# Layer 0's output products of blocks 2 to 7 moved behind its last units and into layer 1, its last half units put in single banks, early steps of the choice cut from ten to six, a scaling split between ScalarE and GpSimd

## The chip, the cores and the metric

The kernel runs on one core of a Trainium2 chip. A core has a matrix engine (TensorE, PE in the profile), a vector engine (VectorE, DVE), an activation engine (ScalarE, ACT), a general engine (GpSimd, POOL) and an engine that issues transfers (SyncE, SP). Each runs its own list of instructions in order; semaphores order the engines against one another. Matmuls write into PSUM, which has eight banks of 128 x 512 fp32 values; everything else is held in SBUF or in device memory. The metric is device time in microseconds, the median over runs.

## The reference

The program is a sequence of four residual layers over x, 8 x 512 tokens of 128 fp32 features. The change touches layer 0 and the start of layer 1. Layer 0 has an attention without softmax and a mixture of experts for each head:

```python
# layer 0, attention: three branches, batch norm over all tokens, a sigmoid as spike
q, k, v = (sigmoid(4.0 * (batch_norm(norm(x) @ W.T) - 1.0)) for W in (Wq, Wk, Wv))
qk = heads(q * k) * 8 ** -0.5                 # 16 heads of 8
x = x + merge(qk @ (heads(v).T @ heads(v))) @ Wp.T + bp

# layer 0, experts: 8 heads of 16 features, 16 experts, the two best are taken
t = (norm(x) @ Wm + bm).reshape(-1, 16)       # one row for each token and head
w = softmax(t @ expert_emb); topw, topi = top_k(w, 2)
hmid = gelu(einsum('td,edi->tei', t, W1) + b1)   # 16 -> 64, all 16 experts
eo = einsum('tei,eio->teo', hmid, W2) + b2       # 64 -> 16
comb = (take(eo, topi) * topw).sum(1).reshape(..., 128)
x = x + comb @ Wo + bo
```

Layer 1 begins with a layer norm of x and a linear attention (q, k through exponentials, a sum over k and v, its product with q, an output product), followed by a feed-forward part. Layers 2 and 3 (softmax attention and low-rank experts; a convolution-like attention and a gated feed-forward part) come after and are not touched.

## The kernel before, in words

The 4096 tokens are 8 blocks of 512 (`NB = 8`, `TB = 512`), and a block is 4 tiles of 128 tokens (`J = 4`, `P = 128`). `x[b]` holds a block with tokens on partitions. The order of the work is written out by hand: each engine does its instructions in the order in which the program names them.

Layer 0 has three parts, by time in the profile. *Pass one* (0 to 41 us) normalizes x, makes the three branches and their statistics. *Pass two* (42 to 101 us) is a software pipeline over the blocks: `run` takes a list of stages with a lag each and calls each with the block number plus its lag. Its `scale(b, J)` makes the normalized input of the experts, four ACT instructions of 128 x 128, one for each tile (`scaled`, L743); with the default `own=3` it would do three on ACT and the fourth on POOL (L349), as pass one does. `turned` transposes the result, `hidden` makes h, `logits` takes the products with the expert vectors, and `exponentials` writes exp(logits) into acc. `biased` (L352) and the product of two spikes (L392) are on POOL.

The *experts* (103 to 382 us) are 128 units, one for each block b and expert e, with n = 16 b + e. The first half of a unit (`first_half`) makes hmid of 64 features for all 8 heads: four matmuls, one into a single bank with the tag "first" and three into a tile of three banks (two such tiles, `threes`, taken in turn), and two gelus on ACT (L569 of 128 x 512, L570 of 128 x 1536). The second half (`second_half`), two units later, multiplies back to 16 features for each head (PE), adds the bias and multiplies by the gate of that expert (DVE, L582, tile pr), and POOL adds pr to acc (L588). For e = 0, DVE writes acc itself. The gates, nonzero for two experts of each token and head, come from `choice(b)`: twelve steps on DVE and POOL (L448 to L474), ending with a transpose and four transfers of `gates[b]` to device memory on SP (L477). `spread(b, k)` then loads the gates of four experts into a tile gs with a copy on each of the 16 partitions of a head (eight transfers, L550; three such tiles). While the units run, `side` lets one step of the next block's choice, and of some preparations for layer 1 (`places`, `first_norms`), be done in each unit; in units 0 and 1 it does five steps each, so that the choice for block 1 is done early.

`finish(b)` makes layer 0's output: acc of a block times Wo, four 128 x 128 matmuls over tokens (`by_token`, L253), and adds it to x[b] on DVE (`add_to_residual`, L274). It runs in the fifth unit of the next block. The product goes to the bank that is the first of the three-bank tile which this unit doesn't use (`banks["own"]`). The very last pr isn't added to acc; it is a second term of the last finish, which thus has eight products. After the last unit the two remaining second halves use the second and third bank of `threes[0]`, and then finish(7) runs.

`layer1` starts with some memsets on POOL (L1245 to L1254; `nought` is a tile of zeros that is copied to device memory), and goes over the blocks with its own list of stages (`stages`, above the loop at its end): transposes (`turn_`), projections (`project_q`, `project_kv`), maps with exponentials (`q_map`, `k_map`), `gather` (the sum over k and v), `attend`, `output`, then the feed-forward part with a lag. PE, ACT and DVE take their shares of a stage in the order of this list. PSUM then has four single banks (tag "one") and two pairs. `late()` holds layers 2 and 3.

SBUF pools matter for where acc lies: `once` lives for layer 0 only, `first` is held until layer 1's end.

Of the kernel before, what the change touches and what calls it, by code (L numbers as in the profile page):

```python
# [17 lines left out]
F32 = mybir.dt.float32  # L18
# [7 lines left out]
P = 128  # L26
D = 128
# [137 lines left out]
def body(ctx, tc, dram, spans, x_in, ib, it, ic, ei, out):  # L165
# [111 lines left out]
        return t[:, j * P : (j + 1) * P]  # L277


    def layer0():  # L280


# [5 lines left out]
        with ExitStack() as st:  # L288
# [4 lines left out]
            emb = once.tile([P, 8, 16], F32, tag="emb", name="emb")  # L293
            emb_f = emb.rearrange("p h e -> p (h e)")
            h = once.tile([P, NB, TB], F32, tag="h", name="h")
            acc = once.tile([P, NB, TB], F32, tag="acc", name="acc")
            depth = once.tile([P, NB, TB], F32, tag="depth", name="depth")
            gates = [tc.dram_tile([P, TB], F32, name=f"gates{b}") for b in range(NB)]
            G = J * 8
# [40 lines left out]
            def stats(b):  # L340
                l0[b]["by"] = stats_of(x[b], J)

            def scale(b, own=3):
                l0[b]["xn"] = xn = norm.tile([P, J, D], F32, tag="xn", name="xn")
                nb, rs = l0[b]["by"]
                scaled(xn, x[b], (nb, rs), own)
                for j in range(own, J):
                    r1, n1 = rs[:, j : j + 1], nb[:, j : j + 1]
                    nc.gpsimd.tensor_scalar(xn[:, j, :], x[b][:, j, :], r1, n1, ALU.mult, ALU.add)  # L349

            def biased(b, bias):
                nc.gpsimd.tensor_tensor(  # L352
# [84 lines left out]
                nc.vector.tensor_tensor(by_expert(depth, b), pl3, over(mx), ALU.subtract)  # L437

            def exponentials(b):
                nc.scalar.activation(acc[:, b, :], depth[:, b, :], AF.Exp)  # L440

            def choice(b):


                d, ex = by_expert(depth, b), by_expert(acc, b)
                place, top, sm = small("place"), small("top"), small("sm")
                eq, one, left = big("eq"), big("one"), big("left")
                nc.vector.scalar_tensor_tensor(eq, d, 0.0, rank, ALU.is_equal, ALU.mult)  # L448
                yield "V"
                nc.vector.tensor_reduce(place, eq, AX.X, ALU.max)  # L450
                yield "V"
                nc.vector.tensor_tensor(one, eq, over(place), ALU.is_equal)
                yield "V"
                nc.vector.scalar_tensor_tensor(left, one, -1e30, d, ALU.mult, ALU.add)
                yield "V"
                nc.vector.tensor_reduce(top, left, AX.X, ALU.max)
                yield "V"
                nc.vector.tensor_tensor(eq, left, over(top), ALU.is_equal)
                nc.gpsimd.tensor_tensor(eq, eq, rank, ALU.mult)
                yield "V"  # L460
                nc.vector.tensor_reduce(sm, ex, AX.X, ALU.add)
                nc.vector.reciprocal(sm, sm)
                nc.gpsimd.tensor_tensor(ex, ex, over(sm), ALU.mult)
                yield "V"
# [24 lines left out]
            with (  # L489
                tc.tile_pool(name="a0h", bufs=1) as hp,  # L490
                tc.tile_pool(name="a0", bufs=2) as ap,
                psum({"one": 8}),
                tc.manual_schedule(),
            ):
                hs = [hp.tile([P, NB, TB], F32, tag=f"h{k}", name=f"h{k}") for k in range(3)]
                bst = [hp.tile([P, NB, 6], F32, tag=f"bst{k}", name=f"bst{k}") for k in range(3)]

                def run(stages, iterations):
                    for i in iterations:
                        for f, lag in stages:  # L500
                            if 0 <= i + lag < NB:
                                f(i + lag)

                run(
                    (
                        (scale, 2),
                        (stats, 3),
                        (turned, 1),
                        (project, 0),
                        (lambda b: biased(b, "bp"), -2),  # L510
                    ),
                    range(-3, NB + 2),
                )
                keep_clock(22)
                sc, bi = batch_norm()
                expand()
                run(
                    (
                        (turned, -2),
                        (lambda b: scale(b, J), -1),  # L520
                        (turn_v, 3),
                        (logits, -3),
                        (attended, 0),
                        (stats, 0),
                        (spikes, 4),
                        (gram, 2),
                        (gram_out, 1),
                        (hidden, -2),
                        (exponentials, -3),
                        (lambda b: chosen(3), -4),  # L530
                        (lambda b: biased(b, "bo"), -1),
                        (lambda b: keep_clock(6), -3 - NB // 2),
                    ),
                    range(-4, NB + 3),
                )
                chosen(20)
# [36 lines left out]
            def second_half(b, e, hm, gs):  # L573
                po = bank()
                for i in range(4):
                    mm(
                        po[32 * i : 32 * (i + 1), :],
                        w2[:, e, :, :].rearrange("p a o -> p (a o)"),
                        hm[:, i, :],
                    )  # L580
                pr = acc[:, b, :] if e == 0 else wp.tile([P, TB], F32, tag="pr", name="pr")
                nc.vector.scalar_tensor_tensor(  # L582
                    pr, po, f0["b2"][:, e : e + 1], gs, ALU.add, ALU.mult
                )
                if (b, e) == (NB - 1, 15):
                    l0[b]["last"] = pr
                elif e > 0:
                    nc.gpsimd.tensor_tensor(acc[:, b, :], acc[:, b, :], pr, ALU.add)  # L588

            def finish(b):  # L590
                terms = [(lambda j: acc[:, b, j * P : (j + 1) * P], f0["wo"])]
                if "last" in l0[b]:
                    terms.append((lambda j: cols(l0[b]["last"], j), f0["wo"]))
                add_to_residual(b, by_token(terms, None))

            def places():

# [45 lines left out]
            with tc.manual_schedule():  # L643
# [36 lines left out]
                def second(n):  # L680

                    if n >= 2:
                        b, e = units[n - 2]
                        second_half(b, e, hms.pop(n - 2), gs[(n - 2) // 4][:, e % 4, :])
                        fetch(n - 1)
                    for _ in range(1 if n > 1 else 5):
                        side("V", n)

                for n in range(len(units) + 2):
                    first(n)  # L690
                    if n >= len(units):

                        banks["own"] = threes[0][:, 1 + n - len(units), :]
                        second(n)
                        banks.pop("own")
                        continue

                    banks["own"] = threes[(n + 1) % 2][:, 0, :]
                    b, e = units[min(n, len(units) - 1)]
                    if e == 4 and b > 0:  # L700
                        finish(b - 1)
                    else:
                        side("P", n)
                    banks.pop("own")
                    second(n)
                finish(NB - 1)
                n = 1000
                while kinds.get(1) != "end":
                    side("V", n)
# [121 lines left out]
    def layer1():  # L831
# [9 lines left out]
        with tc.tile_pool(name="l1", bufs=2) as wp, tc.tile_pool(name="l1c", bufs=1) as once:  # L841
# [372 lines left out]
            def chosen_put():  # L1214
# [11 lines left out]
                (f_scale, -3),  # L1226
                (q_map, 0),
                (project_kv, 0),
                (z_turn, -7),
                (output, -2),  # L1230
                (k_map, 0),
# [7 lines left out]
            with tc.manual_schedule():  # L1239
# [10 lines left out]
                for k, name in enumerate(("eb1", "eb2")):  # L1250
                    lo, hi = spans["rows"][name]
                    nc.sync.dma_start(ebs[:, k, :], dram["rows"][:, lo:hi].partition_broadcast(P))
                nought = once.tile([P, J, D], F32, tag="nought", name="nought")
                nc.gpsimd.memset(nought, 0.0)  # L1254
                for b in range(1, NB):
                    nc.sync.dma_start(
# [1421 lines left out]
```

## Time and profile before

| what | us |
|---|---|
| median of three runs (lowest, highest) | 1400.63 (1397.15, 1401.19) |
| the profiled execution, its own time | 1393.95 |
| its span | 1392.2 |
| layer 0, pass one and pass two | 0 to 101 |
| layer 0, the experts | 103 to 382 |
| layer 1 | about 384 to 510 |
| layers 2 and 3 | about 510 to 1392 |
| PE, ACT, DVE, POOL busy over the span | 1327.5, 1014.6, 1014.3, 642.4 |

The profiled execution is 0.5% below the median of the runs, so sums made from its rows are compared with its own time. A line of the timeline reads: start, length, engine, line of the kernel, operation, what it writes and reads, its shape, how many instructions the line stands for, and in brackets how long the engine had been idle ahead of it and who ended that. Matmuls of fp32 are issued as several passes, so "x8" stands for four matmuls of 128 x 128. The lines of a stretch give the busy time (and instructions) of PE, weight loads, DVE, ACT and POOL, the granted clock of the matrix engine as a fraction, the busy share of the transfer engines, and GB/s. Lines of waits give the engine and line that waited, for what, the sum, how many times, and the longest.

### The profile page before, as it was taken

The numbers are of one execution on the slowest core, as the hardware profiler recorded it, in microseconds if no ns is written. First come the engines' busy times: TensorE is split into PE (matmuls) and PEld (weight loads), VectorE is DVE, ScalarE is ACT, GpSimd is POOL, SyncE is SP. The second block draws the span as 40 slices with busy tenths as digits, with TensorE's granted clock in tenths as the row PEclk, the third lists the DMA queues.
The fourth block names the chain that finished last, engine by engine and source line by source line (L and its number), as shares of the span: only waits on it lengthen the run. The fifth ranks groups of instructions, "written<-read, shape, count | busy, mean of one in ns | idle before, by whom it ended". The sixth has DMA issues, their size and how long they took to land.

```text
span 1392.2 us, 33106 instructions
## 1 busy us (share of the span) xinstructions
PE 1327.5 (95%) x12935; PEld 706.1 (51%) x12935; DVE 1014.3 (73%) x2148; ACT 1014.6 (73%) x2060; POOL 642.4 (46%) x748
## 2 busy tenths in 40 slices
PE   7889999999989999999999999999999999999997
PEld 3762222222267655547447545555555545555576
DVE  6785556666467778863783778888788797887876
ACT  7869999999978656665684686787767867667632
POOL 6645666666632533330472353353443634424432
PEclk9999999999999999999999999999999999999999
DMA  5019999999681010031211101101011010010000
GB/s 180 1 27 139 141 126 127 132 127 133 85 272 32 28 40 24 16 108 33 60 31 38 45 2 22 30 2 33 20 22 24 9 33 20 19 27 9 2 8 16
DMA packets 100713, 78.14 MB, mean 56 GB/s; under 512 B 52717, under 2 KB 93581, under 8 KB 96206
## 3 DMA queue, kind: packets, MB, share of 16 engines
q1 hardware_dynamic: 98828, 72.10, 28.3%
q0 software_dynamic: 1152, 2.36, 0.6%
q8 instruction: 102, 1.67, 0.6%
q10 hardware_dynamic: 578, 1.57, 0.3%
q14 instruction: 53, 0.43, 0.1%
HBM read 59.03 MB, written 16.97 MB: 55 GB/s over the span
## 4 chain that ended last, share of the span: by engine, by line
PE 52%; ACT 22%; DVE 19%; issue 3%; POOL 2%; DMA 1%; SPq 1%; DVEq 0%; ACTq 0%; POOLq 0%
PE ps L250 41%; PE ps L1556 8%; ACT hm L570 6%; ACT ex L1635 5%; DVE nm L1629 5%; ACT hm L569 3%; ACT prod L2023 2%; PE ps L2206 1%; DVE fa L1395 1%; DVE acc L2009 1%; DVE s L732 1%; ACT h L389 1%; DVE fa L1379 1%; DVE fsc L1374 1%; ACT q L1517 1%
## 5 line engine op out<-in xcount | busy, mean ns | idle before, releaser
L1635 ACT ACTIVATE ex<-ps,nm 128x512 f32<-128x512 f32 x512 | 345.2, 687 | 172.6 <-DVE nm L1629 170.2
L1629 DVE TENSOR_REDUCE nm<-ps 128x2 f32<-128x1024 f32 x256 | 301.1, 1211 | 41.9 <-PE ps L250 41.5
L250 PE MATMUL ps<-q,k 64*64 64x512 f32 (+1 forms) x2240 | 258.3, 565 | 7.4 <-ACT ex L1635 5.4
L250 PE MATMUL ps<-ex,vs 128*64 128x512 f32 x1024 | 233.9, 599 | 1.1 <-DVE sm L1649 1.1
L1650 POOL TENSOR_TENSOR vs<-v,sm 128x256 f32<-128x256 f32 x128 | 78.6, 614 | 296.6 <-DVE sm L1649 269.6
L588 POOL TENSOR_TENSOR acc<-acc,pr 128x512 f32<-128x512 f32 x119 | 165.6, 1391 | 93.8 <-DVE pr L582 85.8
L1556 PE MATMUL ps<-xt,blob_a 64*64 64x512 f32 x912 | 207.8, 589 | 0.5 <-SPq L1523 0.5
L570 ACT ACTIVATE hm<-ps,blob_f 128x1536 f32<-128x1536 f32 x128 | 196.2, 1533 | 0.0
L582 DVE SCALAR_TENSOR_TENSOR pr<-ps,blob_f,gs 128x512 f32<-128x512 f32 x120 | 90.1, 750 | 93.7 <-PE ps L250 72.1
L250 PEld LDWEIGHTS ps<-q,k 64*64 64x64 f32 x2240 | 74.6, 132 | 150.5 <-ACT ex L1635 77.6
L250 PE MATMUL ps<-h,w 32*128 32x512 f32 x1024 | 148.3, 643 | 1.1 <-ACT hm L569 0.6
L250 PEld LDWEIGHTS ps<-ex,vs 128*64 128x64 f32 x1024 | 68.1, 137 | 152.9 <-issue 126.7
L250 PE MATMUL ps<-hm,w 128*32 128x512 f32 x1024 | 136.9, 607 | 2.3 <-DVE pr L582 2.2
L2024 POOL TENSOR_TENSOR acs<-acs,prod 128x512 f32<-128x512 f32 x96 | 124.0, 1292 | 23.9 <-ACT prod L2023 19.4
L1556 PE MATMUL ps<-blob_a,ct 64*64 64x128 f32 x1824 | 118.6, 269 | 0.0
L1556 PE MATMUL ps<-blob_a,xt 64*64 64x128 f32 x1824 | 118.6, 269 | 0.0
L1556 PEld LDWEIGHTS ps<-blob_a,ct 64*64 64x64 f32 x1824 | 106.3, 133 | 0.0
L1635 ACT ACTIVATION_READ_ACCUMULATOR ex<-ps,nm 128x1 f32 x512 | 104.9, 205 | 0.0
L1556 PEld LDWEIGHTS ps<-blob_a,xt 64*64 64x64 f32 x1824 | 103.0, 133 | 0.0
L569 ACT ACTIVATE hm<-ps,blob_f 128x512 f32<-128x512 f32 x128 | 88.0, 687 | 13.3 <-PE ps L250 13.2
L250 PEld LDWEIGHTS ps<-h,w 32*128 32x128 f32 x1024 | 41.0, 184 | 109.1 <-ACT hm L569 100.5
L1556 PEld LDWEIGHTS ps<-xt,blob_a 64*64 64x64 f32 x912 | 61.7, 133 | 32.2 <-issue 28.7
(373 smaller groups left out, 2204.5 us busy)
## 6 DMA issues: line engine op xcount, KB each, us to landing
gs<-gates SPq DMA_DIRECT2D x248, 128.0 KB, 7.4
ht<-turned_h SPq DMA_DIRECT2D x20, 180.0 KB, 3.0
turned_h<-hb SPq DMA_DIRECT2D x40, 88.0 KB, 2.3
blob_f<-in_f SPq DMA_DIRECT2D x1, 2560.0 KB, 9.0
blob_a<-in_a SPq DMA_DIRECT2D x1, 2056.0 KB, 13.5
x<-in_x SPq DMA_DIRECT2D x8, 256.0 KB, 5.8
gates<-turned SPq DMA_DIRECT2D x32, 64.0 KB, 4.7
slots_in<-nought SPq DMA_DIRECT2D x8, 256.0 KB, 4.8
```

Source lines behind the costliest of these rows:

```text
L250: nc.tensor.matmul(out_, lhs, rhs, start=start, stop=stop)
L389: nc.scalar.activation(hk, hk, AF.Sigmoid, bias=bi[:, k : k + 1], scale=sc[:, k : k + 1])
L569: nc.scalar.activation(hm[:, 0, :], p1, AF.Gelu, bias=bias)
L570: nc.scalar.activation(hm[:, 1:, :], p3, AF.Gelu, bias=bias)
L582: nc.vector.scalar_tensor_tensor(pr, po, f0["b2"][:, e : e + 1], gs, ALU.add, ALU.mult)
L588: nc.gpsimd.tensor_tensor(acc[:, b, :], acc[:, b, :], pr, ALU.add)
L1556: ins = nc.tensor.matmul(*args, **kw).ins
L1629: nc.vector.tensor_reduce(nm, ps, AX.X, ALU.max, negate=True)
L1635: nc.scalar.activation(ex[kt][:, i, :], ps[:, i, :], AF.Exp, bias=nm[:, i : i + 1], accum_out=sm[:, kt, i : i + 1],)
L1650: nc.gpsimd.tensor_tensor(vs[:, tiles, :, :], vs_[n][:, tiles, :].rearrange("p j (i n) -> p j i n", i=2), sm[:, tiles, :].unsqueeze(3).to_ ...
L2023: nc.scalar.activation(p, src, AF.Copy, scale=w)
L2024: nc.gpsimd.tensor_tensor(t["acs"], t["acs"], p, ALU.add)
```

## The change

acc is no longer one tile: blocks 0 to 2 have a tile each in layer 0's pool, blocks 3 to 7 one tile, `last_acc`, in the pool that lives through layer 1. `finish` moves out of `layer0` so that layer 1 can call it. finish(0) and finish(1) stay in the fifth unit of the next block; finish(2) runs after the last unit's first half, between the two remaining second halves; finish(3) to finish(7) become a stage of layer 1, one in each of the iterations 0 to 4, after `project_kv`. The last pr is added to acc as the others are. The two remaining second halves use the banks "one" and "first". In units 0 and 1 `side` does four and two steps. `scale` always gives its fourth tile to POOL, in pass two too. The tile of zeros uses a buffer of another tile, "zo".

```diff
+    acc = []
+    last_acc = first.tile([P, NB - 3, TB], F32, tag="acc", name="acc")
+
+    def finish(b):
+        wo = f0["wo"]
+        add_to_residual(b, by_token([(lambda j: cols(acc[b], j), wo)], None))
...
-            acc = once.tile([P, NB, TB], F32, tag="acc", name="acc")
+            acc.extend(once.tile([P, TB], F32, tag=f"acc{b}", name="acc") for b in range(3))
+            acc.extend(last_acc[:, b, :] for b in range(NB - 3))
...
-            def scale(b, own=3):
+            def scale(b):
                 l0[b]["xn"] = xn = norm.tile([P, J, D], F32, tag="xn", name="xn")
                 nb, rs = l0[b]["by"]
-                scaled(xn, x[b], (nb, rs), own)
-                for j in range(own, J):
-                    r1, n1 = rs[:, j : j + 1], nb[:, j : j + 1]
-                    nc.gpsimd.tensor_scalar(xn[:, j, :], x[b][:, j, :], r1, n1, ALU.mult, ALU.add)
+                scaled(xn, x[b], (nb, rs), 3)
+                r1, n1 = rs[:, 3:4], nb[:, 3:4]
+                nc.gpsimd.tensor_scalar(xn[:, 3, :], x[b][:, 3, :], r1, n1, ALU.mult, ALU.add)
...
-                        (lambda b: scale(b, J), -1),
+                        (scale, -1),
...
-                if (b, e) == (NB - 1, 15):
-                    l0[b]["last"] = pr
-                elif e > 0:
-                    nc.gpsimd.tensor_tensor(acc[:, b, :], acc[:, b, :], pr, ALU.add)
-
-            def finish(b):
-                terms = [(lambda j: acc[:, b, j * P : (j + 1) * P], f0["wo"])]
-                if "last" in l0[b]:
-                    terms.append((lambda j: cols(l0[b]["last"], j), f0["wo"]))
-                add_to_residual(b, by_token(terms, None))
+                if e > 0:
+                    nc.gpsimd.tensor_tensor(acc[b], acc[b], pr, ALU.add)
...
-                    for _ in range(1 if n > 1 else 5):
+                    for _ in range((4, 2)[n] if n < 2 else 1):
                         side("V", n)
...
                     if n >= len(units):
-
-                        banks["own"] = threes[0][:, 1 + n - len(units), :]
+                        if n > len(units):
+                            banks["own"] = bank("first")
                         second(n)
+                        if n == len(units):
+                            banks["own"] = threes[0][:, 0, :]
+                            finish(2)
                         banks.pop("own")
                         continue
...
-                    if e == 4 and b > 0:
+                    if e == 4 and 0 < b < 3:
                         finish(b - 1)
...
-                finish(NB - 1)
...
                 (project_kv, 0),
+                (lambda b: b > 2 and finish(b), 3),
                 (z_turn, -7),
...
-                nought = once.tile([P, J, D], F32, tag="nought", name="nought")
+                nought = wp.tile([P, J, D], F32, tag="zo", name="nought")
```

More of the change, by code (lines that the diff above doesn't have):

```diff
@@ L439, in exponentials @@
             def exponentials(b):
-                nc.scalar.activation(acc[:, b, :], depth[:, b, :], AF.Exp)
+                nc.scalar.activation(acc[b], depth[:, b, :], AF.Exp)
             def choice(b):
-                d, ex = by_expert(depth, b), by_expert(acc, b)
+                d = by_expert(depth, b)
+                ex = acc[b].rearrange("p (g e) -> p g e", e=16)
                 place, top, sm = small("place"), small("top"), small("sm")
@@ L580, in second_half @@
                     )
-                pr = acc[:, b, :] if e == 0 else wp.tile([P, TB], F32, tag="pr", name="pr")
+                pr = acc[b] if e == 0 else wp.tile([P, TB], F32, tag="pr", name="pr")
                 nc.vector.scalar_tensor_tensor(
```

## The prediction

> **What bounds the kernel now.** I read the page's busy shares, then the busy time by stretches, then ACT's timeline where it stops. Layer 0's experts run from 103 to 382 us. One block, 16 units, there:
>
> ```profile
> core 0: us, PE busy (x) PEld busy (x) DVE busy (x) ACT busy (x) POOL busy (x), PEclk, DMA share, GB/s
> 219.30:253.90 34.60, 34.29 (x268) 8.49 (x264) 24.14 (x49) 33.20 (x32) 23.61 (x18) 1.00 0.99 130
> ```
>
> ACT works 33.2 of 34.6 us, so ACT is the limit and the rest is a stop. The gap and what PE does in it:
>
> ```profile
> 285.33 0.69 ACT L569 ACTIVATE hm<-ps,blob_f 128x512 f32<-128x512 f32 x1
> 285.92 1.53 ACT L570 ACTIVATE hm<-ps,blob_f 128x1536 f32<-128x1536 f32 x1
> 288.82 0.69 ACT L569 ACTIVATE hm<-ps,blob_f 128x512 f32<-128x512 f32 x1 [1.37 <-PE ps L250]
> ```
> ```profile
> 285.82 0.83 PE L250 MATMUL ps<-blob_f,acc 128*128 128x128 f32 x6
> 286.59 1.07 PE L250 MATMUL ps<-hm,w 128*32 128x512 f32 x8
> 287.58 1.14 PE L250 MATMUL ps<-h,w 32*128 32x512 f32 x8
> ```
>
> Units start 2.066 us apart (0.69 and 1.53 less their overlap) except at one place in each block: `finish` of the block before. It writes into a bank of the three-bank tile that the next unit's first half needs, PE waits for DVE's addition (L274), and ACT stops 1.37 us. ACT shows this at 150.04, 184.52, 219.30, 253.91, 288.82, 323.74 and 358.23: seven finishes, blocks 0 to 6.
>
> The next stage, where layer 0 ends:
>
> ```profile
> 384.35 0.49 PE L250 MATMUL ps<-blob_f,acc 128*128 128x128 f32 x2 [0.72 <-POOL acc L588]
> 386.44 0.69 DVE L274 TENSOR_TENSOR x<-x,ps 128x512 f32<-128x512 f32 x1 [1.93 <-PE ps L250]
> 386.60 0.14 POOL L1245 MEMSET v<- 128x4 f32 x2 [2.31 <-PE ps L250]
> 391.13 1.65 ACT L743 ACTIVATE xn<-x,nb,rs 128x128 f32<-128x128 f32 x4
> 391.58 1.13 PE L250 MATMUL ps<-v,k 128*128 128x129 f32 x8 [2.16 <-POOL nb L737]
> ```
>
> The last finish (eight product terms, since the last product isn't added yet) holds PE until 386.4; then POOL clears tiles until 389.3 and only then makes the scale (rs, nb) that ACT and PE wait for. From the fourth iteration of layer 1 on, nothing has slack:
>
> ```profile
> 426.17 1.05 PE L250 MATMUL ps<-blob_l,ot 128*128 128x128 f32 x8
> 427.06 0.60 PE L925 MATMUL ps<-blob_c,o 128*128 128x128 f32 x4
> 427.26 0.69 DVE L274 TENSOR_TENSOR x<-x,ps 128x512 f32<-128x512 f32 x1 [0.42 <-PE ps L250]
> 428.14 0.69 DVE L859 SCALAR_TENSOR_TENSOR k<-ps,ex 128x512 f32<-128x512 f32 x1 [0.19 <-ACT v L877]
> 428.40 0.57 ACT L927 COPY ot<-ps 128x512 f32<-128x512 f32 x1
> ```
>
> **The parts, one by one** (minus is time saved).
>
> *Finishes 2 to 6 leave the stage.* In the changed program's order finish(0) and finish(1) stay where they were, finish(2) comes after unit 126's second half, finish(3) to finish(7) stand in layer 1's iterations 0 to 4, after `project_kv` on PE and after `q_map` on DVE. Five of the seven stops go: 5 x 1.37 = −6.85. What is late next is the gate loads. The DMA share of the stretch above is 0.99. SP's waits from 150 to 382 us:
>
> ```profile
> SPq L550 <- DMA gs<-gates: 67.6, 101, 1.8
> SPq L550 <- DMA gates<-turned: 19.0, 15, 3.1
> SPq L550 <- DVE pr L582: 16.0, 12, 2.2
> ```
>
> The third line is slack: loads that were ready to be issued and had no free buffer. To put a period to it: a gs load lands a median 7.3 us after its issue and about eight are in flight, so the 32 of a block take 4 x 7.3 = 29.2; once a block the rings run empty, because the next loads wait for the gates to be written (337.5 to 340.0 has DMA share 0.18 against 1.11 after it): about 2.1; the gates' own 0.26 MB at 130 GB/s: 2.0. That is 33.3, and ACT's bound is 16 x 2.066 = 33.06. So a block should shrink by 1.37 less 0.2; I give 1.0 of the 6.85 back: −5.85. Bounds: −6.85 if the loads keep up, −2.0 if a block needs 34.3 (eight loads in 7.5 us, the gates and a longer hole), since it is 34.7 now. It can't cost, as these waits exist now too.
>
> *The end of layer 0.* The last units' halves now take the banks "one" and "first" in place of spare banks of the three-bank tile. Second half 126 waits for pr(125), which ends at 381.54, so it starts at 381.6 (before 380.5); finish(2) follows with 1.05 us, then second half 127 at about 383.4 (before 382.54); pr(127) ends near 385.35 (before 384.5). Its addition on POOL is new: 1.28, to about 386.7. But eight products (2.07 us) leave PE: proj_q(0) starts when finish(2)'s addition is done, near 384.4, against 386.24, so −1.85 on PE, and stats(2) on DVE at 385.4 against 387.05. POOL's memsets wait for the last addition: 386.75 against 386.60, so nb(2) and scale(2) come 0.15 later, if anything. In my walk through the waits the head start of PE and DVE wins by the second iteration (k_map(1), at 398.21 now): −2.0. Bounds: −2.0, and +0.15 if the POOL chain keeps setting the start.
>
> *Five finishes in layer 1.* Each is eight PE passes (1.05, as the row at 426.17) and one DVE addition (0.69). PE idles 2.36 us in iteration 0 and 1.98 in iteration 1 ahead of the output product, which hides both there; were that cover gone they would cost 1.05 each. In iteration 2 PE idles 1.0, in 3 and 4 0.6. On DVE the addition stands between q_map and the output's addition, whose product now ends 1.05 later; k_map goes from 428.14 to about 429.0, `turn_o` and the ot copy behind it on ACT by about as much, and ACT's timeline has no idle left there. I take 0.4, 0.9 and 0.9: +2.2. Bounds: 0 if DVE's later idle (1.36 us at 432.14) swallows it, +3.15 (3 x 1.05) if PE is the path.
>
> *The tile of zeros* shares a buffer whose next user comes seven iterations later, behind some 50 us of layer 1, and its copies start where they did: 0; without that cover it would be one memset, 0.52.
>
> *Pass two.* ACT scales three of four tiles (1.65 to about 1.25 us for each block) and POOL one (0.45, as the eight rows of pass one). Early scales, each waiting on POOL's nb (54.40, 58.53, 63.23, 69.99), come forward by about 0.4 with DVE idle 1.80 at 64.12 waiting for what follows: −0.6; from 70 to 94.7 DVE is continuous and hides it; the last scale (93.08) leads to the last logits that DVE waits for: −0.4. Sum −1.0, lower end −1.4. Against it, POOL's tile queues behind L392 and L352 (1.27 each), so it can be later than ACT's fourth was, and POOL runs beside DVE:
>
> ```profile
> 73.82 1.27 POOL L352 TENSOR_TENSOR x<-x,blob_bc 128x512 f32<-128x512 f32 x1
> 74.18 1.46 DVE L452 TENSOR_TENSOR one<-eq,place 128x512 f32<-128x512 f32 x1
> ```
>
> L452 takes 0.68 otherwise; a row at 86.64 (L467, 1.24 against 0.68) looks alike. Both together are 1.34, my upper end: +1.3.
>
> [...]
>
> *Fewer early steps of the choice* (5+5 to 4+2 in units 0 and 1): choice(1) ends in unit 7 rather than 3, and SP writes gates(1) after block 0's last loads, where later blocks write theirs. Now DVE's steps push pr(0) to 108.92 and ACT stops 1.54 at 110.81, but that falls in a stretch at half clock:
>
> ```profile
> 107.14:110.55 3.41, 3.41 (x16) 0.52 (x8) 3.05 (x5) 2.13 (x3) 0.59 (x1) 0.50 0.99 156
> ```
>
> PE's slow passes explain that stop; it stays. The loads of block 0's last group come sooner: pr at 135.25 waited 1.10 for them, which ACT felt as 0.27. I take −0.3; bounds −0.5 and 0 (gates(1) would need to be some 4 us later still before it hurt).
>
> [...]
>
> **Sum:** −5.85 −2.0 +2.2 −1.0 −0.3 = −6.95. The profiled execution took 1393.95 us (span 1392.2), so it becomes 1387.0. The median of the runs is 1400.63 (1397.15 to 1401.19), 0.5% above it; on that scale I forecast 1393.7. Layers 2 and 3 are untouched and begin when layer 1 ends, so I pass the saving on whole.
>
> **Rivals.**
> A. *The gate loads become the bound.* For it: share 0.96 to 0.99 in all six blocks, 101 SP waits for earlier loads. Against: 16.0 us of waits for buffers. With 34.3 us per block the sum is −2.0 −2.0 +2.2 −1.0 −0.3 = −3.1: 1397.5.
> B. *Layer 1 pays more than layer 0 saves* (slower). Each iteration's chain product, addition, output addition, k_map, gather is serial: if all five finishes cost their whole 1.05 + 0.69 plus a bank's wait like layer 0's 1.37, 3.1 each, that is +15.5, and the sum +6.4: 1407. For it: no idle on ACT at 428; the L765 transposes of iterations 3 and 4 wait for the added addition's bank. Against: PE idles 2 us in iterations 0 and 1. It decides above 1.8 us per finish (9.15 saved over five).
> C. *POOL's queue sets both edges.* The fourth tile is late in pass two (+1.3), memsets hold layer 1's start (+0.15), the rest as forecast: −2.5: 1398.1.
> D. *It doesn't do what it says:* block 2's product is still in layer 0's tail, on PE before second half 127. That is counted above, and costs about 0.9 of the layer's end; it changes nothing else.
>
> **Chances.** Forecast, saving over 4.2 us: 0.58; A 0.14; C 0.10; B 0.18, of which a third lies within 4.2 of no change. About 0.3%, 4.2 us, is what a measurement of this kernel can tell from no change. So faster 0.59 (with a little of A), same 0.29, slower 0.12. The forecast's own range is 1389.9 (all lower ends: −6.85 −2.0 +0 −1.4 −0.5 = −10.75) to 1396; with A, C and the near part of B, and the scatter of the runs, 1389 to 1402; outside lie some 0.05 below and 0.12 of B above.
>
> **What would show it.** In the changed profile, ACT's rows at the fifth unit of blocks 3 to 7 without the 1.37, blocks of 33.1 to 33.5 us; if rival A, pr rows that wait for gs. Layer 1: proj_q(0) about 1.85 earlier relative to the last gelu, and iterations 2 to 4 longer than 7.5 us by 0.4 to 0.9; beyond 1.8, rival B. POOL rows of 0.45 in pass two, and the first expert gelu 1.0 us earlier than 103.13. I am wrong if blocks stay at 34.7, or if DVE's rows in pass two lengthen.

## The result

The changed kernel is a little slower, not faster: 1402.85 us (median of 22 runs) against 1399.82 us, a ratio of 1.0025 with a 95% interval of 1.0016 to 1.0034. That is +3.5 us where 6.95 less were forecast, and it lies outside the stated range of 1389 to 1402.

The changed kernel's profiled execution has a span of 1401.9 us, that of before 1392.2 us. These 9.7 us are more than the medians differ: the profiled execution of before, 1393.95 us, is quicker than each of the 22 that it is compared with here (1396.57 to 1401.61). The parts, from the timelines, show where they lie (a block goes from the first gelu of its first unit to that of the next block; "the last gelu" is the start of the last unit's first gelu):

| stretch, us | before | changed | forecast of the difference |
|---|---|---|---|
| to the first gelu of the experts | 103.13 | 102.78 | −1.0 |
| block 0 | 35.15 | 34.37 | −0.3 |
| block 1 | 34.49 | 40.90 | 0 |
| block 2 | 34.78 | 34.49 | 0 |
| blocks 3 to 7, to the last gelu | 172.20 | 167.99 | −5.85 |
| last gelu to the first k of layer 2 (end of layer 0, layer 1) | 122.30 | 126.41 | +0.2 |
| layers 2 and 3 | 890.15 | 894.96 | 0 |

ACT's timeline of the changed kernel, in blocks 1 and 2:

```profile
151.25 0.69 ACT L577 ACTIVATE hm<-ps,blob_f 128x512 f32<-128x512 f32 x1 [5.79 <-PE ps L250]
155.31 0.69 ACT L577 ACTIVATE hm<-ps,blob_f 128x512 f32<-128x512 f32 x1 [1.94 <-PE ps L250]
189.80 0.69 ACT L577 ACTIVATE hm<-ps,blob_f 128x512 f32<-128x512 f32 x1 [1.37 <-PE ps L250]
```

The third is the known stop of a product inside the experts, finish(1). The first is new and four times as long. SP, DVE and PE tell why, in the changed kernel's timeline (SP's lines are issues of transfers; "the rings" stands for the transfers that are issued and have not landed, about eight at a time here):

```profile
126.58 4.55 SPq L485 DMA_DIRECT2D gates<-turned  x4
134.94 24.97 SPq L558 DMA_DIRECT2D gs<-gates  x30
...
146.40 0.75 DVE L590 SCALAR_TENSOR_TENSOR acc<-ps,blob_f,gs 128x512 f32<-128x512 f32 x1 [4.42 <-DMA gs<-gates]
147.21 1.93 PE L250 MATMUL ps<-hm,w 128*32 128x512 f32 x8 [3.95 <-DVE acc L590]
```

and, for comparison, SP and DVE in the kernel before:

```profile
117.83 3.76 SPq L477 DMA_DIRECT2D gates<-turned  x4
122.08 6.36 SPq L550 DMA_DIRECT2D gs<-gates  x8
128.53 28.00 SPq L550 DMA_DIRECT2D gs<-gates  x32
```
```profile
143.39 0.75 DVE L582 SCALAR_TENSOR_TENSOR acc<-ps,blob_f,gs 128x512 f32<-128x512 f32 x1 [0.27 <-DMA gs<-gates]
```

The eight loads at 122.08 are the last group of block 0; in the changed kernel they stand ahead of the gates, not behind them. The writes of block 1's gates were issued 8.8 us later, and the loads that read them began 6.4 us later (134.94 against 128.53). The first product of block 1 waits for them; PE then waits 3.95 us for the bank, and afterwards takes 1.93 us for eight passes that take 1.07 otherwise: PE ran at half clock (0.50) for 6.8 us from 146.2.

From block 3 on, the products' stops are gone, and blocks 3 and 4 take 33.06 and 33.16 us. Blocks 5 and 6 don't; their stretches, with the busy times of PE, weight loads, DVE, ACT and POOL, the clock, the transfers' share and GB/s:

```profile
278.76:312.78 34.02, 33.24 (x260) 7.52 (x256) 23.46 (x48) 33.21 (x34) 23.66 (x18) 1.00 0.97 124
312.78:347.89 35.11, 33.31 (x260) 7.51 (x256) 24.41 (x61) 33.28 (x33) 22.71 (x18) 1.00 0.98 136
```

ACT's work is 33.2 us as it was; the rest is waiting, with the transfer share still at 0.97 and 0.98. DVE's longest waits for a product in the two blocks:

```profile
293.08 0.75 DVE L590 SCALAR_TENSOR_TENSOR pr<-ps,blob_f,gs 128x512 f32<-128x512 f32 x1 [1.60 <-POOL acc L594]
319.85 0.75 DVE L590 SCALAR_TENSOR_TENSOR acc<-ps,blob_f,gs 128x512 f32<-128x512 f32 x1 [2.24 <-DMA gs<-gates]
```

Block 6 waits for gate loads. Block 5 waits for POOL, whose three additions ahead of that took 1.59 to 1.66 us instead of 1.28, beside DVE's last steps of the choice. SP's waits from 150 to 383 us in the changed kernel show the slack in front of the gate buffers fallen from 16.0 to 7.0 us:

```profile
SPq L558 <- DMA gs<-gates: 83.7, 124, 1.8
SPq L558 <- DMA gates<-turned: 20.3, 15, 3.1
SPq L558 <- DVE pr L590: 7.0, 6, 2.3
```

Where layer 0 ends, the changed kernel has

```profile
388.22 0.60 ACT L856 ACTIVATE ex<-ps 128x512 f32<-128x512 f32 x1 [2.51 <-POOL acc L594]
388.24 0.14 POOL L1248 MEMSET v<- 128x4 f32 x2
...
391.92 1.13 PE L250 MATMUL ps<-v,k 128*128 128x129 f32 x8 [1.93 <-POOL rs L246]
```

PE had been early: the projection that stood at 386.24, 6.49 us after the last gelu, is 5.28 us after it now. But ACT's first exponential and the memsets wait for POOL's last addition. The memsets start 7.71 us after the last gelu instead of 6.85, and the sum over k and v comes 11.39 us after it instead of 11.83. Further on, DVE has the output's addition and the k map one after the other as before, only later, since a product stands ahead:

```profile
429.42 0.69 DVE L274 TENSOR_TENSOR x<-x,ps 128x512 f32<-128x512 f32 x1 [0.42 <-PE ps L250]
430.30 0.69 DVE L861 SCALAR_TENSOR_TENSOR k<-ps,ex 128x512 f32<-128x512 f32 x1 [0.19 <-ACT v L879]
```

From the sum over k and v of block 1 to that of block 4, the three intervals are 8.09 us each; in the kernel before they are 7.44 to 7.50.

### The profile page after: what moved, and what is told of

Read it like the earlier page. It is cut to its first block, busy times and chain, and to the rows that moved or that the text cites. A ratio compares the mean times of both kernels' runs of the same rounds, so it can differ in the third digit from the quotient of the medians.

```text
span 1401.9 us, 33085 instructions
## 1 busy us (share of the span) xinstructions
PE 1332.4 (95%) x12927; PEld 708.2 (51%) x12927; DVE 1013.2 (72%) x2148; ACT 1012.9 (72%) x2052; POOL 649.1 (46%) x757
## 3 DMA queue, kind: packets, MB, share of 16 engines
q0 software_dynamic: 1152, 2.36, 0.6%
## 4 chain that ended last, share of the span: by engine, by line
PE 37%; DVE 14%; ACT 10%; issue 2%; POOL 1%; DMA 0%; DVEq 0%; ACTq 0%; POOLq 0%
PE ps L250 27%; PE ps L1559 8%; ACT ex L1638 6%; DVE nm L1632 5%; ACT prod L2026 2%; DVE acc L2012 1%; PE ps L2209 1%; DVE fa L1398 1%; DVE fa L1382 1%; DVE fsc L1377 1%; ACT q L1520 1%; DVE fa L1399 1%; ACT xn L1457 1%; DVE fm L1397 1%; DVE fm L1394 1%
## 5 line engine op out<-in xcount | busy, mean ns | idle before, releaser
L1638 ACT ACTIVATION_READ_ACCUMULATOR ex<-ps,nm 128x1 f32 x512 | 105.2, 206 | 0.0
L1559 PEld LDWEIGHTS ps<-blob_a,xt 64*64 64x64 f32 x1824 | 103.0, 133 | 0.0
```

Source lines behind the costliest of these rows:

```text
L1559: ins = nc.tensor.matmul(*args, **kw).ins
L1638: nc.scalar.activation(ex[kt][:, i, :], ps[:, i, :], AF.Exp, bias=nm[:, i : i + 1], accum_out=sm[:, kt, i : i + 1],)
```

## The experiments

The parts have names here: **E**, early steps 5 + 5 to 4 + 2; **F**, the moved products with the last units' banks and the last addition; **S**, the split of pass two. Ratios are to the kernel before, run on the same chip beside it, with their 95% interval; 0.001 is 1.4 us. There are four groups, each with its own runs of the kernel before: e1 to e4 and e5 to e8 on one chip, e9 to e12 and e13 to e15 on another.

**First, each part alone or left out.**

e1, the changed kernel without E:

```diff
-                    for _ in range((4, 2)[n] if n < 2 else 1):
+                    for _ in range(5 if n < 2 else 1):
```

> The changed kernel with ten early steps of the choice (five and five) as before; all else changed. Theory 1: fewer early steps make the gates of block 1 late; the first product of block 1 waits 4.42 us for its gate loads, ACT stops 5.79 and then 1.94 us in a stretch at half clock, so block 1 takes 40.9 us instead of 34.5. Then this kernel has block 1 near 34.5, no wait of the first product for gs in it, and runs about 6 us below the changed kernel, 2 to 4 us below the kernel before. Theory 2: the loss sits behind layer 1 (layers 2 and 3 took 5.0 us longer in the changed kernel's profile); then block 1 comes back but the time stays at or above the kernel before.

Measured: 0.9973 (0.9959 to 0.9987). Against 1.0025 of the changed kernel that is 7 us, for four steps of the choice. Block 1 took 34.49 us. Theory 1 holds, and theory 2 is out: layers 2 and 3 took 893.1 us in this profile, more than before, in a kernel that is faster.

e2, E alone in the kernel before:

```diff
-                    for _ in range(1 if n > 1 else 5):
+                    for _ in range((4, 2)[n] if n < 2 else 1):
```

> The kernel before with four and two early steps of the choice and nothing else. Theory 1: block 1 gets the stop alone: 4 to 7 us slower than before, the wait of the first product of block 1 for gs near 4.4 us. Theory 2: within 1.5 us of before. My recorded prediction had -0.3 for this part.

Measured: 1.0030 (1.0020 to 1.0041). Block 1 took 40.85 us and block 0 33.46 instead of 35.15. DVE and ACT of e2:

```profile
146.66 0.75 DVE L582 SCALAR_TENSOR_TENSOR acc<-ps,blob_f,gs 128x512 f32<-128x512 f32 x1 [4.50 <-DMA gs<-gates]
151.52 0.69 ACT L569 ACTIVATE hm<-ps,blob_f 128x512 f32<-128x512 f32 x1 [5.88 <-PE ps L250]
```

The same wait, alone: 6.4 us lost in block 1, 1.7 won in block 0, and 4.2 by the ratio.

e3, S alone in the kernel before:

```diff
-                        (lambda b: scale(b, J), -1),
+                        (scale, -1),
```

> The kernel before with the pass-two scaling split between ACT and POOL and nothing else. Recorded prediction: -1.0. Reading of the changed profile: the first gelu came 0.35 earlier (102.78 against 103.13), so -0.4, with the time within 1 us of before; a stretch at half clock may appear in pass two (one did, at 84.7 to 88.2). If POOL's tile costs: +0.5 to +1.3.

Measured: 1.0016 (1.0006 to 1.0026). The first gelu came 0.5 us earlier (102.60), block 0 took 36.13 us instead of 35.15. See e13.

e4, F alone; to the changed kernel with the edit of e1:

```diff
-                        (scale, -1),
+                        (lambda b: scale(b, J), -1),
```

(`scale` itself is as in the kernel before; so it is in e5, e6, e11 and e15.)

> The changed kernel with ten early steps and with pass two scaled by ACT alone: what is left are the moved output products, the last units' banks and the last addition on POOL. From the changed profile: blocks 3 to 7 lost 4.2 us, the end of layer 0 -0.4, layer 1 cost 4.3 up to the first softmax frames, so about 0 against before (-2 to +2). The recorded prediction had -5.65 for these parts. If the loss in layers 2 and 3 belongs to this change, +3 to +5.

Measured: 0.9990 (0.9979 to 1.0002). In its profile blocks 3 to 7 took 166.35 us, 5.85 less than before; the stretch from the last gelu to layer 2 126.14 us, 3.84 more. Of these, −0.8 stands ahead of the first sum over k and v, +1.55 is a half-clock stretch in the first iteration, +1.83 are the three longer intervals, +1.26 comes late in layer 1. So F gains in the experts what was forecast, in this execution, and two thirds of it are lost behind them. Layers 2 and 3 took 892.7 us, less than in e2 and e3, which lack F.

**Then, what sets the price in each place.**

e5, as e4, without the five products in layer 1:

```diff
-                (lambda b: b > 2 and finish(b), 3),
```

> As e4, but layer 1 leaves out the five output products of blocks 3 to 7 and their additions (so that x lacks them). In e4 the iterations 1 to 3 of layer 1 take 8.08 us instead of 7.47, and the time from the last gelu to layer 2's first k is 126.1 us instead of 122.3. Theory 1: the products cost only what these three iterations show, 1.9 us: they return to 7.47, the whole is 1.5 to 2.5 us below e4, and the longer wait of the chosen rows' gather (3.57 us in e4, 2.04 before) stays. Theory 2: they cost all 3.8: then the gather's wait goes back to 2.0 too, and the whole is 3.5 to 4.5 us below e4.

Measured: 0.9990 (0.9977 to 1.0003), as e4. In the profile the three intervals are back at 7.44 to 7.50 us. The gather of the chosen rows, an indirect load that POOL issues late in layer 1, waits 2.0 us again. The stretch to layer 2 is 123.09 us, 0.79 more than before: as in e4, −0.8 ahead of the first sum over k and v and 1.54 for a half-clock stretch in the first iteration. So the profile speaks for theory 2: without the products the stretch is what it was. The medians don't confirm it: e5's blocks 3 to 7 took 169.09 us in its profile, 2.7 more than e4's, so the scatter of the blocks from execution to execution is as large as the effect. The gather's rows from POOL's timeline, and those of the transfers it waits for (six, four of them of 64 KB, with the median time from issue to landing), before and in e4:

```profile
464.74 1.23 POOL L1040 DMA_INDIRECT row<-by_rows,at_int  x1 [2.04 <-DMA by_rows<-fxn]
by_rows<-fxn SPq DMA_DIRECT2D x4, 64.0 KB, 1.6
```
```profile
463.16 1.23 POOL L1043 DMA_INDIRECT row<-by_rows,at_int  x1 [3.57 <-DMA by_rows<-fxn]
by_rows<-fxn SPq DMA_DIRECT2D x4, 64.0 KB, 3.1
```

The last of the transfers it waits for was issued at 462.3 in the first and at 459.2 in the second, so the delay behind it is 2.4 and 4.0 us. The trace has this transfer land 1.6 and 3.1 us after its issue, and POOL begins 0.9 us after that in both, so it is the landing that comes later. All ten profiles with the products in layer 1 have 3.3 to 3.9 in that bracket and a landing after 2.9 to 3.5 us, all seven without have 2.0 and 1.6. Why is open.

e6, as e4, with four groups of gate loads instead of 32:

```diff
-                        gs[k] = spread(k // 4, k % 4)
+                        gs[k] = spread(k // 4, k % 4) if k < 4 else gs[k - 3]
```

> As e4, but only the first four groups of gate loads are made; later units take the gate tiles that are there (so the products are weighted with other gates). It removes 224 of the gs loads. If the loads, and not ACT, set the length of some blocks (33.8 us of block 6 in e4, 34.0 and 35.1 of blocks 5 and 6 in the changed kernel), blocks 3 to 6 all become 33.06 to 33.2 and blocks 1 and 2, with their products still in place, 34.45; the whole is 0.5 to 1.5 us below e4. If ACT and PE set it, nothing moves.

Measured, in four runs: 0.9948 (0.9931 to 0.9965), 5.9 us below e4 by the ratios, where 0.5 to 1.5 were expected. Blocks 4 to 6 took 33.06 to 33.13 us, block 3 33.41. e4's own profile had blocks 3 to 5 at 33.2; it is of one of the quickest of e4's twelve executions (1394.65 us, median 1397.03), so the others probably pay more for the loads than it shows: the profiles of e1, e5, e8 and e11 have blocks of 34.5 to 37.2 us among 4 to 6. Without the loads no block from 3 to 6 is longer than 33.41 us: the loads do set the length of the long ones, though not of each (block 5 of the changed kernel waited for POOL).

e7, the changed kernel with E, where the last group of block 0 is loaded only once block 1's gates are written:

```diff
-                    if k < 4 * NB and k // 4 in written and (k < 3 or 4 * (k - 2) <= done):
+                    if k < 4 * NB and k // 4 in written and (k < 3 or 4 * (k - 2) <= done) and (k != 3 or 1 in written):
```

> The changed kernel with its four and two early steps, but the loads of block 0's last group are issued behind the writes of block 1's gates instead of ahead of them. If the gates of block 1 are late because they stand behind these eight loads on SP and in the rings, the wait of 4.42 us goes down to below 1 us, block 1 is near 34.5 to 35.5 and the whole is 5 to 6 us below the changed kernel. If they are late because the choice itself ends later (turned at 119 instead of 113 us), less than half comes back. Block 0 may wait for its last group instead (0 to 3 us).

Measured: 0.9984 (0.9974 to 0.9993), 5.7 us below the changed kernel. SP in e7:

```profile
119.34 2.60 SPq L485 DMA_DIRECT2D gates<-turned  x4
121.98 34.93 SPq L558 DMA_DIRECT2D gs<-gates  x40
```

(The 40 loads are block 0's last eight and block 1's 32.) With the same four and two steps the gates are issued at 119.3, not 126.6, the first product of block 1 waits 0.27 us, and block 1 takes 35.64 us. Block 0 pays with a wait of 3.28 us for its own last group (36.64 us). So the choice that ends four units later was not the price; that its four small writes now stood behind eight loads, in SP's list and in the rings, was.

e8, as e1, the products in iterations 0, 0, 1, 1 and 2:

```diff
-                (lambda b: b > 2 and finish(b), 3),
+                (lambda b: [finish(k) for k in {0: (3, 4), 1: (5, 6), 2: (7,)}.get(b, ())], 0),
```

> As e1 (ten early steps), but the five output products stand in layer 1's iterations 0, 0, 1, 1 and 2, where PE idles 2.4 and 2.0 us in the profile before, instead of one in each of 0 to 4. If what they cost is PE and DVE time in full iterations, the iterations 1 to 3 (8.08 us in e1) become 7.5 to 7.9 with one at 8.1, 0.8 to 1.5 us below e1, 5 us below the kernel before. If not, the same as e1.

Measured: 0.9988 (0.9976 to 1.0000), not below e1 (0.9973). The first four intervals are 8.08, 8.08, 7.49 and 7.49 us: 0.61 twice, where e1 has it three times, so 0.6 is won in layer 1, somewhat less than expected. In the same profile block 6 took 36.78 us (a product waits 2.53 us for gs, and there is a half-clock stretch at 318). The scatter of the blocks covers the gain.

**A version from these readings.** The loads of a block's first group wait for its gates, and from block 2 on these are issued behind the last eight loads of the block before. e9 is e1 with the choice of blocks 2 to 7 begun four units earlier, which puts the writes ahead of these eight:

```diff
-                choices = [(choice(b), 16 * (b - 1) - 5) for b in range(1, NB)]
+                choices = [(choice(b), 16 * (b - 1) - 9) for b in range(1, NB)]
```

> As e1, with the choice for blocks 2 to 7 begun four units earlier, so that SP issues each block's gates ahead of the loads of the last group of the block before instead of behind them (24 loads, gates, 8 loads in place of 32 loads, gates). Theory: in e1 the loads set blocks 5 and 6 (34.6, 34.5 us), because once a block the rings run empty while the gates land (2 us), and e6, without loads, was about 6 us below e4. Then blocks 3 to 6 become 33.06 to 33.3, and the whole is 2 to 4 us below e1. Rival: the loads' rate itself is too low; then blocks 5 and 6 stay above 34 and the whole is as e1.

Measured: 0.9956 (0.9940 to 0.9971), 2.4 us below e1 by the ratios; the intervals of the two overlap, so the times alone don't settle it. The profiles do: blocks 3 to 6 took 33.07, 33.45, 33.19 and 33.27 us, and blocks 3 to 7 164.8 us to the last gelu, as in e6 without the loads (164.6), where e1 has 168.5. SP's waits from 150 to 372 us in e9:

```profile
SPq L558 <- DVE pr L590: 57.1, 16, 4.6
SPq L558 <- DMA gs<-gates: 17.7, 32, 0.9
```

The rows are turned over: SP now waits 57.1 us for free buffers and 17.7 us for loads; the wait for written gates is no longer in the list. After block 0, where one waits 1.82 us, no product waits more than 0.32 us for gs in this profile. The rings could carry the work all along; the order of 4 transfers among 32 made them the bound.

e10, e9 with the packed products of e8:

```diff
-                (lambda b: b > 2 and finish(b), 3),
+                (lambda b: [finish(k) for k in {0: (3, 4), 1: (5, 6), 2: (7,)}.get(b, ())], 0),
```

> As e9, with the products in layer 1's iterations 0, 0, 1, 1 and 2 as in e8. Layer 1's iterations 2 and 3 at 7.49 as in e8: 0.6 us below e9; stage of the experts as e9.

Measured: 0.9955 (0.9939 to 0.9971): as e9, the third and fourth interval at 7.48 and 7.50. What 0.6 us are worth can't be told at this interval.

e12, the edit of e9 alone in the kernel before:

```diff
-                choices = [(choice(b), 16 * (b - 1) - 5) for b in range(1, NB)]
+                choices = [(choice(b), 16 * (b - 1) - 9) for b in range(1, NB)]
```

> The kernel before, with the choice for blocks 2 to 7 begun four units earlier as in e9 and nothing else. In the kernel before a block takes 34.7 us, 1.37 of it for the product, and its loads keep up; so nothing is gained: within 1 us of before. If loads already cost time there in many executions, 1 to 3 us below.

Measured: 1.0007 (0.9997 to 1.0016), no gain, blocks at 34.5 to 34.9. As long as the products' stops are there the loads keep up; by these ratios F and the earlier gates are worth more together than apart.

**Last, the split.**

e11, the changed kernel without S:

```diff
-                        (scale, -1),
+                        (lambda b: scale(b, J), -1),
```

> The changed kernel with pass two scaled by ACT alone: early steps and moved products as in the changed kernel. It tells what the split is worth beside the other parts. From e1 against e4 (-2.4 us by medians) the split helps and this kernel is 1 to 3 us above the changed one; from e3 (+2.2 against before) it hurts and this kernel is 1 to 3 us below. From the profiles, where the split brings the first gelu some 1.5 us forward and block 0 takes 1.2 us longer, since its products then wait for gate loads: within 0.7 us of the changed kernel.

Measured, in seven runs: 1.0046 (1.0029 to 1.0064), above the changed kernel (1.0025), as e1 against e4 would have it.

e13, e3 once more, with the same edit:

```diff
-                        (lambda b: scale(b, J), -1),
+                        (scale, -1),
```

> The kernel of e3 (the kernel before with the split alone) once more, on another chip or day: e3 had 1.0016 [1.0006, 1.0026]. If the split alone truly costs, 1.001 to 1.002 again; if e3 was the scatter of executions, 0.999 to 1.0005. In the profile I expect the first gelu at 101.7 to 102.8 and block 0 at 35.7 to 36.5.

Measured: 1.0003 (0.9993 to 1.0012). First gelu at 102.91, block 0 at 36.60 us.

e14, E and S without F; to the kernel before:

```diff
-                        (lambda b: scale(b, J), -1),
+                        (scale, -1),
...
-                    for _ in range(1 if n > 1 else 5):
+                    for _ in range((4, 2)[n] if n < 2 else 1):
```

> The kernel before with the split and the four and two early steps: products where they were. Sum of e2 and e3: 1.0046. If the split helps beside the early steps as in the changed kernel against e11: 1.001.

Measured: 1.0016 (1.0005 to 1.0027). Against e13 that is 1.8 us for E, where e2 had 4.2. SP has the same order as in the changed kernel (loads of block 1 from 134.18), but block 0 took 35.87 us, 1.5 more than there, so the first product of block 1 was due later and waited 1.15 us; blocks 5 and 6 took 36.58 and 36.13 us. So the price of E is no constant: 1.8 (e14 against e13), 4.2 (e2), 7 (the changed kernel against e1) and 7.8 us (e11 against e4).

e15, e9 without S; to e9:

```diff
-                        (scale, -1),
+                        (lambda b: scale(b, J), -1),
```

> As e9 without the split (pass two scaled by ACT alone). If the split is worth what e1 and e4 show, 1.7 thousandths above e9, 0.997 to 0.998; if it is worth only what the profiles show at the end of block 0 (0.3 us), as e9 to 0.0005: 0.9955 to 0.996.

Measured, in five runs: 0.9941 (0.9928 to 0.9954), the lowest ratio here, 8.3 us below the kernel before; its interval overlaps e9's.

So S has been added in six places: +0.0016 and +0.0003 to the kernel before, −0.0014 beside E, −0.0017 beside F, −0.0021 beside both, +0.0015 in e9. There is no sign that holds, and each of these differences has an uncertainty of some 0.001 to 0.002 (three of them compare kernels of different groups). What the profiles say is the same in all of them. From the end of pass one (DVE's last `bmv`) to the first gelu, all nine kernels with S took 61.9 to 62.0 us and seven of the eight without 63.1 (e4, with a half-clock stretch at 96.0, 64.8): S shortens pass two by 1.2 us. Pass one ended between 39.4 and 41.0 us, whatever the edit, which hides part of it: the first gelu of kernels with S came at 101.7 to 102.9 us, without S (but for e11, at 102.5) at 103.0 to 104.5, and block 0, with ten early steps, then took 35.4 to 36.6 us instead of 33.9 to 35.2. DVE's row in e1 shows the reason for the second: a product of block 0 waits 2.42 us for its group of gate loads at 134.90, as one waited 1.10 at 135.25 before. Most of the gain of S goes to the wait for loads that didn't start earlier: from the end of pass one to the end of block 0 the kernels with ten early steps took 97.2 to 98.5 us with S and 97.9 to 98.7 without.

## Why the prediction was wrong, step by step

*Fewer early steps: −0.3, bounds −0.5 and 0.* This is the step that failed. The text saw that gates(1) would be written "after block 0's last loads, where later blocks write theirs" and dismissed it with "would need to be some 4 us later still before it hurt". No row stood behind that figure. The rows for it were in the profile: SP's lines at 117.83, 122.08 and 128.53 with the first product of block 1 at 143.39 and 0.27 us of wait there, loads that take 7.3 us to land with eight in flight, and gates that stand in the same rings. Gates put behind eight more loads were issued 7.2 us later (126.58 in the changed kernel, 119.34 in e7), and the loads that read them began at 134.94 instead of 128.53. The term was put at −0.3; it measured +4.2 us alone (e2) and 7 us beside the other parts (e1), with 1.8 in the weakest case (e14).

*Finishes out of the experts: −6.85, 1.0 given back.* The mechanism was right: the stops went. The 1.0 was the weak term: over the profiles with F and late gates (changed kernel, e1, e4, e5, e7, e8, e11), blocks 3 to 7 took between 166.35 and 172.98 us, that is −5.85 to +0.8 against 172.20, where the forecast had −5.85 and said that this part can't cost. e6 shows that the loads make the difference and e9 that their order with the gates does. Rival A, with 0.14, was this; it was right for this term, and the working that put it aside counted a block's loads at 33.3 us by a median landing time, with nothing for its scatter.

*The end of layer 0: −2.0.* Measured −0.44 (sum over k and v 11.39 us behind the last gelu, before 11.83), −0.8 in e4. I had the memsets' 0.15 as the other bound (they came 0.86 later) and chose the head start of PE and DVE; but ACT's first exponential also waits for POOL's last addition (2.51 us in the row above), which this change made one longer. Of the two ends, the one called "if the POOL chain keeps setting the start" was nearer.

*Five finishes in layer 1: +2.2.* The three longer intervals make 3 x 0.61 = 1.8, near the forecast. What was not forecast is 1.3 us at the gather of the chosen rows, 50 us further on, and half-clock stretches at layer 1's start (e1, e4) or in its second half (the changed kernel, 1.4 us). With the small gain ahead of it the whole stretch was 4.1 us longer in the changed kernel and 3.8 in e4. Rival B asked for 1.8 us for each finish; it came to 0.8. The 2.36 and 1.98 us named as PE's idle time are those of its weight loads, ahead of the sum over k and v; PE's own rows there have 2.16 and 1.77.

*The split: −1.0.* Right for pass two, where it is −1.2 in every profile. The first gelu came earlier by only 0.35 in the changed kernel, whose pass one happened to end 0.8 later (40.8 against 40.0), and by up to 1.4 elsewhere; what was not forecast is that block 0's loads took most of it back. The cost that I feared for DVE did not come: L460 and L475 took 1.47 and 1.24 us as before. POOL's tile did cost once: one of the eight, at 75.11 beside L460, took 0.88 instead of 0.45.

*Layers 2 and 3 untouched: 0.* They are, but their time isn't constant: 889.3 to 895.6 us over the profiles, with no relation to the edit (895.5 in e2, 889.9 in e14). The profile of before, 890.15, was at the low end; the 4.8 us by which the two profiles differ here are as much as two waits on DVE differ that the last section shows (2.4 us each), and these don't go with the edit.

## What to carry to other kernels

Where small writes and large loads share a queue and one of the loads reads what the small ones write, the place of the small ones in the queue's order is a step of the critical path (here it was worth 5.7 us, e7 against the changed kernel): count how many loads stand ahead of them, times the interval at which loads are worked off (about 1 us here: nine were issued in 8.8 us from 117.0 in the changed kernel), before moving the work that produces them. A resource that shows a busy share of 0.97 with some slack must be given its scatter, not its median, when a stop beside it is taken away; and the cure may be its order and not its volume (e9). Before moving work to where an engine idles, look for what else has to be over before the next stage can begin (here one addition on POOL).

## What the runs showed of the hardware

In the profiles of before, the changed kernel and e15, the stretches at half clock (0.50) last 3.41 or 6.83 us: 3.41 us at 107.1 in the kernel before, 3.41 us at 84.7, 105.2, 473.9 and 811.8 and 6.83 us at 146.2 in the changed kernel, 3.4 us at 385.4 and 6.8 us at 467.3 in e15. One more, at 1390.6 in the kernel before, is still on when the program ends. In the changed kernel the starts at 84.7, 105.2 and 146.2 lie 20.5 and 41.0 us apart, about 6 and 12 times 3.41. Its stretch of 6.83 us begins within PE's wait of 3.95 us in block 1, and what ACT lost there is more than the wait: 5.79 and 1.94 us for 4.42 us on DVE. In e2 it is 5.88 and 1.80 us for 4.50 us.

In layer 2, DVE's addition of a bias starts late at the same two places, with the same instructions and nothing that the profile names as the reason. From the changed kernel's DVE timeline:

```profile
680.02 0.69 DVE L1506 TENSOR_TENSOR v<-ps,blob_bc 128x512 f32<-128x512 f32 x1 [4.01 <-PE ps L250]
797.80 0.69 DVE L1506 TENSOR_TENSOR v<-ps,blob_bc 128x512 f32<-128x512 f32 x1 [3.99 <-PE ps L250]
```

PE's product had been done at 677.3. In the kernel before both waits are 1.58 us, and so they are in e13, e14 and e15; in e1 to e12 they are 2.6 to 4.1, whatever the edit. They don't go with the kernel, since e3 and e13 are the same one (4.03 and 1.58 us at the first place), nor with the chip alone, since e9 to e12 ran on the same chip as e13 to e15. That is one more reason to compare only runs of one group. What holds DVE there was not tried.
